# beta1 times the features: summed in PSUM by a product with a scaled identity, and z written by ScalarE

## The chip, the cores and the metric

One core of one Trainium2 chip runs the kernel. The metric is the device time of one execution in microseconds, the median of several runs. Engine names as in the profile: PE is TensorE (PEld its weight loads), DVE is VectorE, ACT is ScalarE, POOL is GpSimd, SP is SyncE. A letter L with a number is a line of the kernel before.

## What is computed

32 entries of 512 nodes with 256 features each, one adjacency matrix `adj` of 512 x 512 for all of them, four graph layers in a row, all in f32. Cut to what matters:

```
# layer 0 and, with other weights, layer 3 (B entries, h_t is [B, 512, 256])
pre_u, pre_v = h_t @ W1[:d], h_t @ W1[d:]
hidden = relu(pre_u[:, :, None] + pre_v[:, None] + b1)       # for every pair u, v
S = sigmoid(hidden @ W2 + b2)
a_t = einsum('buv,bud->bvd', S * A, h_t)                     # A = adj
m_t = einsum('uv,bud->bvd', A, h_t) * h_t
z_t = beta1 * h_t + beta2 * (a_t @ Wa + ba) + beta3 * (m_t @ Wm + bm)
# layer 1
z + relu((A @ z) @ W.T + b)
# layer 2: attention of all nodes, softmax(leaky_relu(f1_i + f1_j) + A), + input
```

The change is in the last line of layer 0, the sum z_t.

## The kernel before

`adj` is sparse, and the pair term `hidden` is needed only where `adj` is not zero. The kernel counts the nonzeros, and since they fit, takes the sparse path (`Sparse`); `dense_path` stands for other inputs and does not run here.

The 32 entries go in eight groups of four (`NB = 4`), and each group passes through these stages:

- `first`: transposes the features (hT), computes pre_u and pre_v and writes them as rows of a table in memory (L587).
- `edges` for layer 0 and again for layer 3: 36 blocks a group (`ITEMS`). For each block POOL gathers 128 rows of the table (L612), DVE adds the other side's rows (L691) and does relu and the weighting by W2. For every second block DVE weights all four entries in one operation (L699), and ACT then sums each entry's part (L677, four ACTIVATEs a block); for the others DVE does weighting and sum in four operations (L707). Then come the sigmoid (L597 on ACT, L601 to L641 on DVE) and a scatter of the values to memory (L606, POOL). The row buffers are five, and a gather is issued three blocks ahead.
- `middle`: layers 0 to 2 for the four entries one after another (`middle_one`), and at its end pre_u and pre_v of layer 3.
- `last`: the sums of layer 3 and the output.

`middle_one` is where the change lies. The features stand transposed: feature on the partition, node along the row, in two halves of 128 features (`DC = 2`). For one entry:

1. mhT, that is (A^T h) * h transposed, from PE products and a DVE multiplication by hT (L755).
2. For each half c a bank of PSUM, pz, takes four products with hWa, which is h @ (beta2 Wa), and flat, the matrix S * A of this entry (L845).
3. For each half, ACT writes beta1 * hT + bias into zT (L850; zT is the same buffer as hT), PE adds two products with beta3 Wm to pz (L852), and DVE adds pz to zT (L853). zT is z_t, transposed.
4. zW = z @ W of layer 1: eight products, first those of half 0 and then those of half 1 (L866), brought out by two copies on ACT (L870). Then the products with adjT (called from L875, recorded as L45 with `adjT,zW`), relu on ACT (L876), and the sum with zT on DVE (L877). Layer 2 follows with feats (L888).

The stages of different groups are woven together: while the middle of group t runs, the edges of group t + 1 and of layer 3 of group t - 1, and `first` and `last` of neighbours, are issued between its pieces. `sparse_path` gives each stage's pieces a time, `weave` issues them in the order of these times, and at the places where a piece says that PE will have to wait (`yield True`) it puts in pieces of `first` or `last` as filler. The pieces' times are numbers in the source; the order in which each engine takes its instructions is fixed when the program is built. Each engine takes its own queue in that order. So L853 stands in DVE's queue between operations of the edge stage, and L870 and L850 stand in ACT's queue between sums L677.

The weights times their beta are made once, in `gnn_scaled`; `bcol` there is beta2 ba + beta3 bm as a column.

Of the kernel before, what the change touches and what calls it, by code (L numbers as in the profile page):

```python
# [8 lines left out]
F32 = mybir.dt.float32  # L9
BF16 = mybir.dt.bfloat16  # L10
I32 = mybir.dt.int32
AF = mybir.ActivationFunctionType
ALU = mybir.AluOpType
# [3 lines left out]
P = 128  # L17
# [30 lines left out]
class Model:  # L48
# [48 lines left out]
    def gnn_first(self, L):  # L97
        nc, a, const = self.nc, self.a, self.const
        w = {"L": L}
        w["W1"] = self.load(f"{L}_W1", [P, 2 * DC, D], a[f"{L}_W1"].rearrange("(c p) k -> p c k", p=P))  # L100
        w["b1bc"] = self.bcast(f"{L}_b1", D)
        w["W2bc"] = const.tile([P, D], F32, name=f"{L}_W2bc")
        nc.scalar.dma_start(w["W2bc"], a[f"{L}_W2"].rearrange("k o -> (k o)").partition_broadcast(P))
        w["b2"] = self.bcast(f"{L}_b2", 1)
        w["nb2"] = const.tile([P, 1], F32, name=f"{L}_nb2")
        w["bcol"] = const.tile([P, DC, 1], F32, name=f"{L}_bcol")
        if L == "L3_gnn":
            w["bbc"] = const.tile([P, D], F32, name=f"{L}_bbc")
        for key in ("Wa", "Wm"):
            w[key] = const.tile([P, DC, D], F32, name=f"{L}_{key}")  # L110
        return w
# [14 lines left out]

    def gnn_scaled(self, w, beta, biases):
        nc = self.nc
        for key, n in (("Wa", 2), ("Wm", 3)):
            nc.vector.tensor_scalar(w[key], w[key], beta[n], None, ALU.mult)  # L130
            col, bc = biases[key]
            if n == 2:
                nc.vector.tensor_scalar(w["bcol"], col, beta[n], None, ALU.mult)
                nc.vector.tensor_scalar(w["bbc"], bc, beta[n], None, ALU.mult)
            else:
                nc.vector.scalar_tensor_tensor(w["bcol"], col, beta[n], w["bcol"], ALU.mult, ALU.add)
                nc.vector.scalar_tensor_tensor(w["bbc"], bc, beta[n], w["bbc"], ALU.mult, ALU.add)
# [281 lines left out]
class Sparse:  # L419
# [25 lines left out]
    def psum(self):  # L445
        return self.ps.tile([P, N], F32, name="pst", tag="pst")
# [383 lines left out]
    def middle_one(self, g0, g3, b, i, SA, keep, given):  # L830
        nc, m, w = self.nc, self.m, g0.w
        act, small, psum = self.act, self.small, self.psum
        h, hT, hWa, flat = keep
        if given:
            hWa, mhT = given[b]
# [3 lines left out]
        zT = hT  # L839
        sums = []  # L840
        for c in range(DC):
            cs = slice(c * P, (c + 1) * P)
            pz = psum()
            for r in range(NC):
                nc.tensor.matmul(pz, hWa[:, r, cs], flat[:, r, :], start=(r == 0), stop=False)  # L845
            sums.append(pz)
            yield
        for c, pz in enumerate(sums):
            cs = slice(c * P, (c + 1) * P)
            nc.scalar.activation(zT[:, c, :], hT[:, c, :], AF.Identity, bias=w["bcol"][:, c, :], scale=w["beta1"])  # L850
            for d in range(DC):
                nc.tensor.matmul(pz, w["Wm"][:, d, cs], mhT[:, d, :], start=False, stop=(d == DC - 1))  # L852
            nc.vector.tensor_tensor(zT[:, c, :], zT[:, c, :], pz, ALU.add)  # L853
            yield c == DC - 1
        more = b < NB - 1
        if more:
# [4 lines left out]
        for d in range(DC):  # L861
            for c, pw in halves:
                for k in range(2):
                    cs = slice((c + k) * P, (c + k + 1) * P)
# [21 lines left out]
        for r in range(DC):  # L886
            for ic, pn in enumerate(pns):
# [4 lines left out]
                    start=(r == 0),  # L892
                    stop=(r == DC - 1),
# [37 lines left out]
        for c in range(DC):  # L931
            cs = slice(c * P, (c + 1) * P)
# [435 lines left out]
```

## Time and profile before

| what | value |
|---|---|
| runs shown | 3096.97, 3109.6, 3116.11 us; median 3109.6 |
| profiled execution | 3114.49 us, span 3112.8 us |
| PE busy | 2713.5 us, 87% of the span |
| DVE busy | 2302.9 us, 74% |
| POOL busy | 1531.2 us, 49% |
| ACT busy | 1337.7 us, 43% |
| mean granted PE clock | 0.942 |
| L850 (ACT, 64 times) | 0.810 us each |
| L853 (DVE, 64 times) | 0.678 us each |
| L876 (ACT out of PSUM, 64 times) | 0.682 us each |

Busy is the time in which an engine has an instruction in it. A row of the timeline gives the start, the length, engine and line, the tile written and those read, how many instructions were merged, and in brackets how long the engine stood idle before it and what ended that. A row of the waits gives who waited for whom, the sum in us, how many times, and the longest. One f32 product appears as two instructions on PE.

The middle of the first group begins at about 235 us (the first L845 is at 239.8), and the last middle ends at 2889 us. Up to the first the setup and the first edge stage run, and behind the last the edge stage of layer 3 for the last group. Between them an entry of `middle_one` takes 80 to 94 us, measured from one entry's first L845 to that of the next, in the groups that run with other stages beside them.

### The profile page before, as it was taken

The numbers are of one execution on the slowest core, as the hardware profiler recorded it, in microseconds if no ns is written. First come the engines' busy times: TensorE is split into PE (matmuls) and PEld (weight loads), VectorE is DVE, ScalarE is ACT, GpSimd is POOL, SyncE is SP. The second block draws the span as 40 slices with busy tenths as digits, with TensorE's granted clock in tenths as the row PEclk, the third lists the DMA queues.
The fourth block names the chain that finished last, engine by engine and source line by source line (L and its number), as shares of the span: only waits on it lengthen the run. The fifth ranks groups of instructions, "written<-read, shape, count | busy, mean of one in ns | idle before, by whom it ended". The sixth has DMA issues, their size and how long they took to land. (4 is left out here: it accounts for less than half of the span.)

```text
span 3112.8 us, 32475 instructions
## 1 busy us (share of the span) xinstructions
PE 2713.5 (87%) x8645; PEld 1639.7 (53%) x8646; DVE 2302.9 (74%) x6027; ACT 1337.7 (43%) x4101; POOL 1531.2 (49%) x1328
## 2 busy tenths in 40 slices
PE   6367878889998899989998899989998899879957
PEld 3133444446654566446654565545654466546636
DVE  6964877888689776988489785888679795772761
ACT  3553454444344433444354442544345343443440
POOL 2561553656345552656346562555436563450461
PEclk9688889999999999999999999999999999999979
DMA  8774657776778757776678766787578766551753
GB/s 278 267 238 151 210 164 242 248 261 214 225 214 293 220 189 227 245 263 216 210 212 258 236 196 211 243 266 234 177 225 273 247 220 200 182 183 49 231 196 115
DMA packets 302719, 679.40 MB, mean 218 GB/s; under 512 B 52672, under 2 KB 170944, under 8 KB 294336
## 3 DMA queue, kind: packets, MB, share of 16 engines
q0 software_dynamic: 122688, 414.40, 42.6%
q1 hardware_dynamic: 160880, 225.62, 22.0%
q10 hardware_dynamic: 18960, 37.24, 3.2%
q8 instruction: 70, 1.15, 0.1%
q14 instruction: 121, 0.99, 0.1%
HBM read 531.12 MB, written 146.01 MB: 218 GB/s over the span
## 5 line engine op out<-in xcount | busy, mean ns | idle before, releaser
L606 POOL DMA_INDIRECT cells<-s,cell x576 | 686.4, 1192 | 747.0 <-DMA cells<-s,cell 388.5
L612 POOL DMA_INDIRECT rows<-table,iv x552 | 667.6, 1209 | 619.9 <-DMA table<-puv 150.5
L691 DVE TENSOR_TENSOR rows<-rows,mine 128x1024 f32<-128x1024 f32 x552 | 667.4, 1217 | 191.7 <-DMA rows<-table,iv 173.3
L677 ACT ACTIVATE rows<-rows 128x256 f32<-128x256 f32 x1088 | 439.8, 407 | 506.6 <-DVE rows L699 477.3
L45 PE MATMUL pst<-adj,h 128*128 128x512 f32 x1024 | 452.6, 594 | 0.3 <-PE pst L946 0.3
L707 DVE SCALAR_TENSOR_TENSOR rows<-rows,L_gnn_W2bc 128x256 f32<-128x256 f32 x1120 | 415.0, 417 | 1.8
L45 PE MATMUL pst<-L_gnn_Wa,hT 128*128 128x256 f32 x1024 | 261.3, 406 | 104.8 <-DMA hT<-xT 56.2
L699 DVE SCALAR_TENSOR_TENSOR rows<-rows,L_gnn_W2bc 128x1024 f32<-128x1024 f32 x272 | 329.7, 1214 | 0.3
L45 PEld LDWEIGHTS pst<-adj,h 128*128 128x128 f32 x1024 | 193.4, 191 | 223.3 <-issue 219.4
L45 PEld LDWEIGHTS pst<-L_gnn_Wa,hT 128*128 128x128 f32 x1024 | 204.8, 205 | 151.8 <-issue 85.1
L45 PE MATMUL pst<-eT,feats 128*128 128x512 f32 x512 | 230.9, 604 | 13.0 <-ACT eT L958 13.0
L866 PE MATMUL pst<-WT,hT 128*128 128x256 f32 x512 | 155.1, 470 | 96.0 <-DVE hT L853 96.0
L45 PE MATMUL pst<-adjT,zW 128*128 128x512 f32 x512 | 227.7, 597 | 3.8 <-ACT zW L870 3.8
L1006 PEld LDWEIGHTS pst<-hWa,SA 128*128 128x128 f32 x896 | 213.8, 328 | 7.7 <-issue 4.1
L1006 PE MATMUL pst<-hWa,SA 128*128 128x256 f32 x896 | 216.8, 398 | 0.0
L814 ACT COPY flat<-SA 128x512 f32<-128x512 f32 x128 | 137.7, 1127 | 165.9 <-PE pst L45 83.7
L677 ACT ACTIVATION_READ_ACCUMULATOR rows<-rows 128x1 f32 x1088 | 205.4, 189 | 0.0
L845 PE MATMUL pst<-flat,hWa 128*128 128x512 f32 x448 | 196.8, 592 | 0.0
L866 PEld LDWEIGHTS pst<-WT,hT 128*128 128x128 f32 x512 | 121.4, 242 | 136.6 <-DVE hT L853 107.1
L579 DVE TENSOR_TENSOR puv<-pst,bc_L_gnn_b 128x256 f32<-128x256 f32 x256 | 104.4, 414 | 95.8 <-DMA table<-puv 58.6
L580 ACT COPY puv<-pst 128x256 f32<-128x256 f32 x256 | 93.5, 370 | 180.6 <-DVE puv L579 162.7
L45 PEld LDWEIGHTS pst<-eT,feats 128*128 128x128 f32 x512 | 97.2, 193 | 127.5 <-issue 109.4
(172 smaller groups left out, 3984.4 us busy)
## 6 DMA issues: line engine op xcount, KB each, us to landing
table<-puv SPq DMA_DIRECT2D x256, 256.0 KB, 5.7
SA<-cells POOLq DMA_DIRECT2D x64, 1024.0 KB, 7.2
h<-in_x_dram SPq DMA_DIRECT2D x64, 512.0 KB, 6.5
mine<-table SPq DMA_DIRECT2D x64, 512.0 KB, 5.5
hT<-xT SPq DMA_DIRECT2D x36, 512.0 KB, 5.0
h<-x2s SPq DMA_DIRECT2D x36, 512.0 KB, 4.4
xT<-hT ACTq DMA_DIRECT2D x32, 512.0 KB, 6.1
x2T<-yT SPq DMA_DIRECT2D x32, 512.0 KB, 5.5
```

What stands on the lines that cost most here:

```text
L45: nc.tensor.matmul(out, lhsT, rhs, start=(n == 0), stop=(n == len(pairs) - 1))
L579: nc.vector.tensor_tensor(puv[:, 0, :], pp[:, 0:D], w["b1bc"], ALU.add)
L606: self.nc.gpsimd.indirect_dma_start(out=g.cells[half], out_offset=bass.IndirectOffsetOnAxis(ap=at, axis=0), in_=s, in_offset=None)
L612: self.nc.gpsimd.indirect_dma_start(out=rows, out_offset=None, in_=g.table, in_offset=bass.IndirectOffsetOnAxis(ap=at, axis=0))
L677: self.behind(nc.scalar.activation(part, part, AF.Identity, accum_out=g.s[:, k, b : b + 1]))
L691: self.behind(nc.vector.tensor_tensor(rows, rows, other, ALU.add))
L699: nc.vector.scalar_tensor_tensor(by_entry, by_entry, 0.0, w2, ALU.max, ALU.mult)
L707: nc.vector.scalar_tensor_tensor(part, part, 0.0, w["W2bc"], ALU.max, ALU.mult, accum_out=at)
L814: self.nc.scalar.copy(flat[:, r, :], SA[r][:, :, b])
L845: nc.tensor.matmul(pz, hWa[:, r, cs], flat[:, r, :], start=(r == 0), stop=False)
L866: nc.tensor.matmul(pw[:, at], zT[:, d, cs], m.WT_1[:, d, :], start=(d + k == 0), stop=(d * k == 1))
L1006: nc.tensor.matmul(pz[:, k * D : (k + 1) * D], SA[r][:, cs, b], hWa[:, r, :], start=(r + k == 0), stop=False)
```

## The change

A constant is added for layer 0: `beta1_I`, the 128 x 128 identity times beta1, made once in `gnn_scaled`. In `middle_one` each bank pz starts with a product of `beta1_I` with the half of hT, so that beta1 * h is in the sum that PE makes. The ACTIVATE that wrote beta1 * hT + bias ahead of the sum, and the DVE sum behind it, are gone; in their place one ACTIVATE reads pz when its last product is in, adds the bias, and writes zT.

```diff
@@ gnn_first
-        if L == "L3_gnn":
+        if L == "L0_gnn":
+            w["beta1_I"] = const.tile([P, P], F32, name=f"{L}_beta1_I")
+        else:
             w["bbc"] = const.tile([P, D], F32, name=f"{L}_bbc")
@@ gnn_scaled
+        if "beta1_I" in w:
+            nc.vector.tensor_scalar(w["beta1_I"], self.ident, w["beta1"], None, ALU.mult)
@@ middle_one
         for c in range(DC):
             cs = slice(c * P, (c + 1) * P)
             pz = psum()
+            nc.tensor.matmul(pz, w["beta1_I"], hT[:, c, :], start=True, stop=False)
             for r in range(NC):
-                nc.tensor.matmul(pz, hWa[:, r, cs], flat[:, r, :], start=(r == 0), stop=False)
+                nc.tensor.matmul(pz, hWa[:, r, cs], flat[:, r, :], start=False, stop=False)
             sums.append(pz)
             yield
         for c, pz in enumerate(sums):
             cs = slice(c * P, (c + 1) * P)
-            nc.scalar.activation(zT[:, c, :], hT[:, c, :], AF.Identity, bias=w["bcol"][:, c, :], scale=w["beta1"])
             for d in range(DC):
                 nc.tensor.matmul(pz, w["Wm"][:, d, cs], mhT[:, d, :], start=False, stop=(d == DC - 1))
-            nc.vector.tensor_tensor(zT[:, c, :], zT[:, c, :], pz, ALU.add)
+            nc.scalar.activation(zT[:, c, :], pz, AF.Identity, bias=w["bcol"][:, c, :])
             yield c == DC - 1
```

## The prediction

> **What bounds the kernel now.** I read the page's busy shares first, then what TensorE waited for, then the timelines around the longest of those waits, entry by entry.
>
> ```profile
> PE 2713.5 (87%) x8645; PEld 1639.7 (53%) x8646; DVE 2302.9 (74%) x6027; ACT 1337.7 (43%) x4101; POOL 1531.2 (49%) x1328
> ```
>
> TensorE is the fullest queue, VectorE next. In six stretches of 360 us from 500 to 2660 us PE is busy 332 to 339 us each, so a longer PE queue has little room. The waits of PE, longest in total:
>
> ```profile
> PE pst L866 <- DVE hT L853: 96.0, 22, 9.5
> PE pst L45 <- DMA hT<-xT: 56.2, 4, 28.7
> PE pst L45 <- DMA hT<-x2T: 42.4, 4, 19.2
> PE pst L957 <- DVE ex L918: 41.0, 23, 8.3
> ```
>
> The first is the wait that the change takes aside: the products of z with WT_1 (L866) wait 22 times for VectorE's sum (L853), 96 us. The timelines show why VectorE was late, here in entry 10 (the third of its group of four); PE, then DVE, then ACT:
>
> ```profile
> 1008.69 3.60 PE L852 MATMUL pst<-mhT,L_gnn_Wm 128*128 128x512 f32 x8
> 1012.13 1.89 PE L45 MATMUL pst<-L_gnn_Wa,hT 128*128 128x256 f32 x8
> 1023.54 6.70 PE L866 MATMUL pst<-WT,hT 128*128 128x256 f32 x16 [9.53 <-DVE hT L853]
> 1030.08 1.89 PE L45 MATMUL pst<-L_gnn_Wa,hT 128*128 128x256 f32 x8
> 1031.81 7.03 PE L45 MATMUL pst<-adjT,zW 128*128 128x512 f32 x16
> ...
> 1021.67 1.22 DVE L691 TENSOR_TENSOR rows<-rows,mine 128x1024 f32<-128x1024 f32 x1 [9.14 <-DMA rows<-table,iv]
> 1022.81 0.68 DVE L853 TENSOR_TENSOR hT<-hT,pst 128x512 f32<-128x512 f32 x1
> 1028.13 1.22 DVE L691 TENSOR_TENSOR rows<-rows,mine 128x1024 f32<-128x1024 f32 x1 [1.44 <-DMA rows<-table,iv]
> 1029.27 1.22 DVE L699 SCALAR_TENSOR_TENSOR rows<-rows,L_gnn_W2bc 128x1024 f32<-128x1024 f32 x1
> ...
> 1029.07 0.59 ACT L870 COPY zW<-pst 128x512 f32<-128x512 f32 x1 [14.41 <-PE pst L866]
> 1030.52 0.42 ACT L677 ACTIVATE rows<-rows 128x256 f32<-128x256 f32 x1 [0.87 <-DVE rows L699]
> 1032.13 0.56 ACT L870 COPY zW<-pst 128x512 f32<-128x512 f32 x1
> ```
>
> L853 stands in VectorE's queue behind a gathered block of the edge stage (L691), and that block's DMA landed late. It is not arithmetic that is slow: L853 itself takes 0.68 us. And L866 took 6.70 us for 16 instructions, where after no wait it takes 3.62: PE ran slow after standing still. The wait repeats by place in the group (the gaps before L866 from the PE timeline, entries 4 to 31): first entries mostly 2.8 to 5.7 us, second 3.7 to 3.9, third 5.0 to 9.5, fourth none.
>
> **Two rules of the skill.** The Trainium skill, "TensorE: Matmul & The Clock Gate", section "What's actually happening", says that PE's clock is halved when it has been idle for a while and comes back after some 3.4 us of work. The trace agrees: after a gap of 2.84 us L866 steps at 216 ns, after gaps of 3.3 us or more at 427 ns for up to 13 instructions (some 5.8 us with the first, longer than the page's figure; I go by the trace). Over all L866 groups the steps above 216 ns sum to 39 us, so I count stall and clock apart: 96 + 39 us hang on this wait. "Perfetto Trace Analysis", "Tensor Engine Instruction (MATMUL, LD_WEIGHTS)", says that ACT and DVE take their instructions strictly in order; the L853 row above (late behind L691 though its product had long ended) shows that for DVE, and the forecast uses it for ACT.
>
> **The change, part by part.**
> 1. TensorE, added: 64 products (32 entries, two halves) of 128x512. One f32 product is two instructions (L845: 512 instructions for 256 products), and L845 steps at 429 ns, so 0.86 us each, 1.72 us an entry, 55 us in all. They stand first in the PSUM group and need only hT, which L755 has already used: no new wait.
> 2. VectorE, removed: 64 x 0.678 us (L853) = 43 us, 1.36 us an entry.
> 3. ScalarE: 64 x 0.810 us (L850, out of SBUF) go, 64 come that read PSUM with a bias; nearest row L876, the same shape out of PSUM, 0.682 us. 8 us less on an engine 43% busy: nothing. What matters is its place: the wait for DVE's mhT (L850, 71.8 us of ACT idling) goes, one for PE's last L852 comes. Behind it stand the sums L677.
> 4. Setup: one VectorE operation of 128x128; an L707 of twice that width takes 0.42 us. Nothing.
>
> So the question is where PE waits next. In the order of the changed program I counted, for each entry, how many groups of sums (L677, one group to a gathered block) stand ahead of the new ACTIVATE and ahead of zW's copies (L870), and read in the trace when those sums ended. PE's order is otherwise unchanged around it. The ACTIVATE stands ahead of the late block, so z is ready in time nearly everywhere. But both copies of zW now stand one group of sums later in third entries: before, the first copy stood ahead of that group.
>
> *Third entries (6, 10, 14, 18, 22, 26).* Entry 10: PE would reach the adjT products at 1014.0 + 1.72 + 3.45 (L866) + 1.7 (filler) = 1021; the sums ahead of zW end at 1032.2 in the trace (their L691 at 1028.13 waits for its own DMA, so VectorE's saved time does not help); the copy ends 0.7 later, 1032.9. Before, these products began at 1031.81. So 1.1 us later, and now they, not L866, run at half clock: the slow time of about 5.8 us costs half of itself, 2.9. Sum +4.0. The same reading gives +4.6, +3.8, +4.4, +5.1 for entries 6, 14, 18, 26 and about +3 for entry 22: **+25 us**. The added products vanish in the wait; the wait itself stays, one step further on.
>
> *First entries.* Entry 20: arrival 1914.2 + 1.72 = 1915.9, sums ahead end 1916.4, z at 1917.1, L866 at 1917.2, not 1918.0: 0.8 gained, a stall of 1.3 that leaves the clock full, 3.0 more. Entries 12, 16, 24 give -3.6, -2.3, -0.9; entry 4 is held by zW (-1.1), entries 8 and 28 had no stall (+1.7, +1.5): **-8.5 us**. VectorE has room: it idles 2.8 us for PE at L877 in these.
>
> *Second entries.* PE gains about 2.1 + 2.4 - but VectorE is busy 82.3 to 82.6 of 86 to 88 us in entries 9, 13, 17, 25, so PE waits for it a little later (L957). I count only VectorE's own 1.4 us in five entries, +1 in entry 5, nothing in 29: **-6 us**.
>
> *Fourth entries.* PE never waits in them and VectorE idles 28 to 32 us: 7 x 1.72 = **+12 us**.
>
> *First group (0 to 3).* Waits of 0, 1.7, 0.9, 0: **+4.2 us**.
>
> Sum: 25 - 8.5 - 6 + 12 + 4.2 = +26.7 us. The profiled execution took 3114.5 us (span 3112.8), so 3141; the median of the runs shown is 3109.6, 4.9 less, so **3136 us**, 0.85% more.
>
> Bounds: what the trace does not show is the gathers' pace once PE runs differently. If the third entries' blocks come as before but the clock survives, +25 becomes +8; if second entries get all of PE's gain, -6 becomes -22. Both give 3136 - 33 = 3103. If first and second entries gain nothing and pay 1.72 each, +26.7 becomes 25 + 12 + 4 + 24 = 65: 3175.
>
> **The rivals.**
> *A, faster: the wait really goes.* Mechanism: in third entries the blocks ahead of zW come some 11 us earlier, because ScalarE no longer idles 71.8 us behind mhT and gives row buffers back sooner (POOL waited 70.4 us for L677). Then all 96 + 39 is won and 55 paid: 3109.6 - 80 = 3030. It decides when the sums ahead of zW end before PE gets to the adjT products (1021 in entry 10, they end at 1032). Against: the block was issued only when POOL was done waiting for scatters to land ahead of an SA load (4.02 us), which the change does not touch.
> *B, slower by the full product cost.* 55 us on a full PE and new waits as long as the old: 3165. For: PE is 93% busy from 500 to 2660. Against: stalls at that very place swallow a part.
> *C, no change.* Gathers and VectorE pace the loop, PE's 55 us fill its idle time, VectorE's 43 us help a little: 3110, within 15. For: PE idles 399 us of the span. Against: fourth entries have no idle PE.
> *D, the new ACTIVATE is not where it should be.* In the built order it follows directly on sums that end before z is due; excluded but for two or three entries.
>
> **How the numbers follow.** Forecast 0.55, C 0.16, B 0.16, A 0.13. The forecast alone is 3115 to 3155. A difference of about 1% is what a measurement of this kernel can tell from none. Slower by more than that is over 3141: a little under half of the forecast (0.26) and B (0.16), 0.42. Faster is A, 0.13; the rest, 0.45, is within 1%. The range runs from 3095 (the lower bound, with some of A) to 3165 (B).
>
> **What would show it.** Right: L866's wait falls from 96 to below 25 us; PE waits appear at the adjT products for zW (L870), 8 to 12 us long, once in a group, with those products slow behind them; PE busy up by some 40 us; fourth entries longer by 1.7 us; the same row waits (L691) of 8 to 9 us. Wrong: zW's copies not waiting for sums in third entries (A), or second entries shorter by over 3 us (VectorE was not the limit), or waits growing elsewhere in first entries.

## The result, and the profile after

The changed kernel took 3147.9 us (median of 4 runs, 3140.4 to 3156.4), the kernel before 3111.0 in the same job: ratio **1.0147, 95% interval 1.0121 to 1.0173**. That is slower by 37 us; the forecast was 3136 us, and its terms added up to 26.7 us more. The profiled execution has a span of 3143.8 us, 31.0 more than before; the mean granted clock is 0.941 for 0.942. Lines of the kernel after stand four further down (L866 is L870, L870 is L874, L691 is L695, and so on); the new product is L848, the new ACTIVATE L857.

The page's busy line after:

```profile
PE 2758.8 (88%) x8773; PEld 1653.3 (53%) x8774; DVE 2270.7 (72%) x5964; ACT 1324.0 (42%) x4101; POOL 1540.8 (49%) x1328
```

PE is busy 45 us longer (forecast: some 40 visible) and still has 12% of the span idle, so the added work alone doesn't explain the time. What PE waited for (total us, times, longest):

```profile
PE pst L45 <- ACT zW L874: 52.7, 7, 12.2
...
PE pst L961 <- DVE cols L921: 38.3, 6, 11.4
PE pst L961 <- DVE ex L922: 32.6, 14, 6.8
...
PE pst L870 <- ACT hT L857: 6.2, 3, 2.9
```

The wait of the products with WT_1 has gone, from 96.0 us to 6.2. In its place PE waits before the products with adjT, for zW. Entry 10 again (third of its group), PE, DVE and ACT of the kernel after:

```profile
1032.81 3.62 PE L870 MATMUL pst<-WT,hT 128*128 128x256 f32 x16
1036.26 1.89 PE L45 MATMUL pst<-L_gnn_Wa,hT 128*128 128x256 f32 x8
1047.36 8.74 PE L45 MATMUL pst<-adjT,zW 128*128 128x512 f32 x16 [9.21 <-ACT zW L874]
...
1036.91 1.23 DVE L695 TENSOR_TENSOR rows<-rows,mine 128x1024 f32<-128x1024 f32 x1 [8.99 <-DMA rows<-table,iv]
...
1042.26 1.23 DVE L695 TENSOR_TENSOR rows<-rows,mine 128x1024 f32<-128x1024 f32 x1 [1.40 <-DMA rows<-table,iv]
1043.40 1.22 DVE L703 SCALAR_TENSOR_TENSOR rows<-rows,L_gnn_W2bc 128x1024 f32<-128x1024 f32 x1
...
1031.28 0.69 ACT L857 ACTIVATE hT<-pst,L_gnn_bcol 128x512 f32<-128x512 f32 x1 [1.03 <-PE pst L856]
1044.65 0.42 ACT L681 ACTIVATE rows<-rows 128x256 f32<-128x256 f32 x1 [12.68 <-DVE rows L703]
...
1046.74 1.06 ACT L874 COPY zW<-pst 128x512 f32<-128x512 f32 x2
```

z is written early (1031.28) and L870 runs without a wait at full clock, 3.62 us. But both copies of zW (1046.74) stand behind a group of sums L681 (1044.65), and VectorE reaches the weighting that those sums need (1043.40) only behind the same late gathered block (8.99 us) that z waited for before, and the next one (1.40 us). PE stands still for 9.21 us and then runs the adjT products slowly, 8.74 us for 16 where before it took 7.03. This much went as forecast.

Time by place in the group tells the rest. The table has the mean length of an entry (from its first product with flat to that of the next entry), entries 8 to 27, five at each place, read from the PE timelines; "before" has two columns, the profile shown and that of a second run of the same kernel (the first experiment):

| place | before, two runs | after | after less their mean |
|---|---|---|---|
| first | 89.7, 88.9 | 87.0 | -2.3 |
| second | 87.2, 87.7 | 91.6 | +4.2 |
| third | 88.2, 85.9 | 90.3 | +3.3 |
| fourth | 92.0, 90.9 | 92.0 | +0.6 |

The sum is +5.7 us a group (357.1 and 353.4 before, 360.9 after), and second entries carry most of it. The forecast had them shorter. In a second entry PE's waits add up to 12.5 us after the change and to 11.6 and 10.6 us in the two runs before. So of the 4.2 us some 1.4 are more waiting, though the wait for z is gone; 1.7 are the product's own time, which the waits do not swallow here; and the other 1.1 are slower steps of PE (7.3 us a second entry over what the same steps take at full clock, and 5.4 and 6.9 us in the two runs before).

### The profile page after: what moved, and what is told of

It is laid out like the page before. It is cut to its first block, busy times and chain, and to the rows that moved or that the text cites. A ratio compares the mean times of both kernels' runs of the same rounds, so it can differ in the third digit from the quotient of the medians.

```text
span 3143.8 us, 32632 instructions
## 1 busy us (share of the span) xinstructions
PE 2758.8 (88%) x8773; PEld 1653.3 (53%) x8774; DVE 2270.7 (72%) x5964; ACT 1324.0 (42%) x4101; POOL 1540.8 (49%) x1328
## 3 DMA queue, kind: packets, MB, share of 16 engines
q8 instruction: 71, 1.16, 0.1%
## 5 line engine op out<-in xcount | busy, mean ns | idle before, releaser
L610 POOL DMA_INDIRECT cells<-s,cell x576 | 693.7, 1204 | 769.8 <-DMA cells<-s,cell 369.0
L695 DVE TENSOR_TENSOR rows<-rows,mine 128x1024 f32<-128x1024 f32 x552 | 667.3, 1218 | 237.1 <-DMA rows<-table,iv 218.2
L681 ACT ACTIVATE rows<-rows 128x256 f32<-128x256 f32 x1088 | 440.3, 407 | 673.0 <-DVE rows L703 641.2
L45 PE MATMUL pst<-adjT,zW 128*128 128x512 f32 x512 | 238.9, 622 | 61.9 <-ACT zW L874 52.7
L681 ACT ACTIVATION_READ_ACCUMULATOR rows<-rows 128x1 f32 x1088 | 205.5, 189 | 0.0
L45 PEld LDWEIGHTS pst<-adjT,zW 128*128 128x128 f32 x512 | 101.3, 200 | 187.7 <-issue 120.4
L579 PE MATMUL pst<-w_L_gnn_W,hT 128*128 128x512 f32 x256 | 140.0, 674 | 37.7 <-ACT hT L566 20.0
```

What stands on the lines that cost most here:

```text
L45: nc.tensor.matmul(out, lhsT, rhs, start=(n == 0), stop=(n == len(pairs) - 1))
L579: nc.tensor.matmul(pp, hT[:, 0, ks], w["W1"][:, 0::DC, :], start=True, stop=False)
L610: self.nc.gpsimd.indirect_dma_start(out=g.cells[half], out_offset=bass.IndirectOffsetOnAxis(ap=at, axis=0), in_=s, in_offset=None)
L681: self.behind(nc.scalar.activation(part, part, AF.Identity, accum_out=g.s[:, k, b : b + 1]))
L695: self.behind(nc.vector.tensor_tensor(rows, rows, other, ALU.add))
```

## Experiments

Twelve kernels; each ratio is against the kernel before on the same chip, with its 95% interval.

**1. The kernel before again**, to see how far two profiles of one program differ.

> The kernel before, unchanged, for a second trace of it. Ratio 1.000 within 0.003. Every theory: the wait of L866 for L853 is 90 to 100 us again, in first, second and third entries, none in fourth. If the two short groups of the first trace (entries 8 to 11 and 24 to 27, 350 us against 360 for the others) are chance, other groups are the short ones here.

1.0013 (0.9998 to 1.0029). Its groups differ from the first profile's by up to 10 us; single entries are compared as means over five only, and differences of a place below some 2 us are not read.

**2. The product alone.** A product of a zero matrix with hT is put first in each bank, z stays on ScalarE and VectorE:

```diff
+            nc.tensor.matmul(pz, w["none"], hT[:, c, :], start=True, stop=False)
```

> The kernel before with one product more per bank, of a zero matrix with hT, so 55 us more for TensorE and everything else as it was. Theory 1 (an added product costs only in entries where TensorE does not wait anyway): 12 us from fourth entries, 4 from the first group, 2 to 8 from third entries, whose first copy of zW falls one group of sums later in the built order here too: 18 to 25 us, ratio 1.006 to 1.008. Rival B (TensorE is full): 55 us, 1.018. Rival C (the chain of gathers and scatters paces a group of four): 0 to 8 us, below 1.003.

1.0012 (0.9999 to 1.0026): a miss for my theory. 55 us of PE work cost about 4 us, no more than the unchanged kernel differed from itself in run 1. First entries got shorter with it, 87.0 us for 89.3: in the kernel before, four of the five stand 2.8 to 3.7 us at L866, and behind the longer three of these waits it runs slowly; here the product fills that time and no wait is left. Why the block that held z also comes earlier there isn't settled.

**3. ScalarE's part alone.** The new ACTIVATE without the product; z leaves out beta1 * h.

```diff
-            nc.scalar.activation(zT[:, c, :], hT[:, c, :], AF.Identity, bias=w["bcol"][:, c, :], scale=w["beta1"])
-            nc.vector.tensor_tensor(zT[:, c, :], zT[:, c, :], pz, ALU.add)
+            nc.scalar.activation(zT[:, c, :], pz, AF.Identity, bias=w["bcol"][:, c, :])
```

> The changed kernel without its product: beta1 times h is left out of z, ScalarE writes z out of PSUM. Theory 1 (the wait moves from L866 to the products with adjT in third entries, and what first entries gain is given back in second ones): between -10 and +10 us, ratio 0.997 to 1.003, with 50 to 60 us of waiting for zW. Rival B (the product is all that the change costs, 55 of TensorE against 37 measured): -18 us, 0.994. Rival A (the wait is gone): -80 us.

1.0050 (1.0022 to 1.0078). The wait for zW is here too, 74.9 us.

**4. The product, with VectorE writing z.** As after, but z = pz + bias by one VectorE operation:

```diff
-            nc.scalar.activation(zT[:, c, :], pz, AF.Identity, bias=w["bcol"][:, c, :])
+            nc.vector.tensor_scalar(zT[:, c, :], pz, w["bcol"][:, c, :], None, ALU.add)
```

> The changed kernel with VectorE in ScalarE's place: z = pz + bias by one VectorE operation, the product kept, no ScalarE operation on z. Theory 1 (as in the run with the product alone: the wait for VectorE at L866 is back, the product lies in it): 15 to 25 us, 1.005 to 1.008, so some 15 us below the changed kernel. If ScalarE's place in the queue costs nothing, it is as slow as the changed kernel: 37 us, 1.012 or more.

1.0013 (1.0000 to 1.0026). Same products, same PE work as after, but none of the loss: entries 87.0, 86.1, 87.9, 92.0. So in this order of the queues the loss of the changed kernel hangs on z being written by ScalarE and not by VectorE, and the product adds to it only then (1.0050 without it, 1.0147 with it).

**5 and 6. The order of ScalarE's queue.** In the order built for the changed kernel, the second relu of y and the copies of feats in second entries stand behind one more group of sums than before. I took that for the cause. `behind` orders an instruction of the edge stage behind the middle stage's last instruction but one on its engine; here sums and block adds follow the last one, which puts relu and feats one group earlier again. Run in the changed kernel and, as a control, in the kernel before:

```diff
-    def behind(self, ins):
+    def behind(self, ins, back=2):
-        if len(names) > 1 and names[-2]:
+        if len(names) >= back and names[-back]:
-            self.tc.add_manual_dep(ins.ins, names[-2], order, reason="behind the middle stage")
+            self.tc.add_manual_dep(ins.ins, names[-back], order, reason="behind the middle stage")
-                self.behind(nc.scalar.activation(part, part, AF.Identity, accum_out=g.s[:, k, b : b + 1]))
+                self.behind(nc.scalar.activation(part, part, AF.Identity, accum_out=g.s[:, k, b : b + 1]), 1)
-            self.behind(nc.vector.tensor_tensor(rows, rows, other, ALU.add))
+            self.behind(nc.vector.tensor_tensor(rows, rows, other, ALU.add), 1)
```

> The changed kernel with the edge stage's sums (ScalarE) and block sums (VectorE) ordered behind the last piece of the middle stage instead of the last but one. In the built order the second relu and the feats copies of second entries then stand behind one group of sums less, as in the kernel before; third entries keep both copies of zW behind the late group. Theory 2 (the 4 us that second entries lost are this place in ScalarE's queue): 18 to 28 us below the changed kernel, 1.004 to 1.009 of before, second entries back at 87 to 88 us. Rival (the product's time on TensorE is what second entries pay): second entries stay at 91 to 92 us, 1.012 to 1.015.

> The same order rule in the kernel before, as a control of the rule alone. The wait for L853 in third entries is untouched, the relu and sum of y stand one or two blocks earlier. Theory 2: -10 to +5 us, 0.997 to 1.002. If the rule by itself is worth as much as in the changed kernel (18 us or more), the run with the changed kernel says nothing of the changed kernel's own place in the queue.

1.0071 (1.0043 to 1.0099) and 0.9970 (0.9954 to 0.9986). Second entries fell to 88.5 us. That looked like a confirmation; runs 11 and 12 undid it.

**7 and 8. The sums ahead of zW held back.** Besides the order of 5 and 6, in third entries the sums between z and zW are issued one block later:

```diff
+        self.hold = b == 2
...
-            if summed:
+            if summed and self.hold:
+                late.append(summed.pop(0))
+            elif summed:
                 summed.pop(0)()
```

> As the changed kernel with that order rule, and in third entries the one group of sums that comes between z and zW is issued a block later, so that both copies of zW stand ahead of the late group. Theory 2 (in third entries the wait for the late block was handed from z to zW by ScalarE's queue): the wait of the adjT products for zW falls from 53 us to under 10, third entries are 4 to 7 us shorter than with the rule alone, 25 to 40 us in all: 0.992 to 1.001 of before. Rival (the late block holds third entries up wherever it is waited for): no more than 5 us below the run with the rule alone, with a new wait at the next products, for y.

> Both order edits in the kernel before, the control of the run above. VectorE's sum for z stands behind the late block there, so the copies of zW cannot come early: within 0.003 of the kernel before with the rule alone, by theory 2 and by the rival alike.

1.0163 (1.0133 to 1.0193) in the changed kernel, a miss, and 0.9947 (0.9922 to 0.9972) in the kernel before. PE's waits in run 7 (its line numbers; L888 adds z to y, L968 turns the attention weights):

```profile
PE pst L968 <- DVE ex L929: 72.7, 31, 8.9
...
PE pst L899 <- DVE yT L888: 35.0, 14, 4.7
```

The wait for zW is gone, and PE waits two steps further, at y and at the attention weights; third entries grew to 94.3 us. The late block is waited for wherever its work next stands ahead of the middle stage. In the kernel before, the same hold did no harm (0.9947, and 0.9970 without it in run 6).

**9 and 10. Which half of the change costs under the order of 5 and 6.** Run 9 is the kernel of run 4, run 10 that of run 3 (z leaves out beta1 * h), both with that order:

> The product of beta1 stays, VectorE writes z out of PSUM, ScalarE has no part in it, and sums and row adds follow the last mark (the order rule of the e5 and e6 runs, 1.0071 and 0.997). Theory 1, the forecast's own terms hold once the order is fixed and add up: the product alone costs its 1.72 us in fourth entries (12 us in all), so 1.000 to 1.003, fourth entries 92.0 us, third entries at about 86 us as in e6, because L870 waits for VectorE and zW does not. Rival, the two parts cost only together: 0.995 to 0.998, what fourth entries lose comes back in first ones (87 us instead of 89).

> ScalarE writes z from PSUM, without the product (z leaves out beta1*h), and sums and row adds follow the last mark. Theory 1, terms add up: third entries pay for the wait on zW as in e5 (about 90 us against 86 in e6, some 28 us in all), first and second entries as e6 or a little shorter, fourth 90.3 us: 1.002 to 1.006. Rival, the two parts cost only together: 0.996 to 0.999, third entries at 86 to 88 us.

1.0115 (1.0093 to 1.0137) and 1.0001 (0.9988 to 1.0013). Both miss both of their theories: run 10 lies between its two ranges, with third entries of 87.1 us and second ones of 91.9; run 9 lies far above, and third entries took 93.4 us. Its DVE and PE in entry 18:

```profile
1784.97 1.23 DVE L695 TENSOR_TENSOR rows<-rows,mine 128x1024 f32<-128x1024 f32 x1 [6.68 <-DMA rows<-table,iv]
...
1793.68 1.12 PE L961 MATMUL pst<-ident,ex 128*128 128x128 f32 x4 [4.26 <-DVE ex L922]
```

One block later than the one that z waits for, VectorE stands 6.68 us for a gather with the softmax behind it. The costs of the parts don't add up, and which part costs more turns round with the order of the queues (runs 3 and 4 against 10 and 9).

**11 and 12. The order mended in second entries alone**, from y to the copies of feats; ScalarE's order in all other entries stays that of the changed kernel.

```diff
-                self.behind(nc.scalar.activation(part, part, AF.Identity, accum_out=g.s[:, k, b : b + 1]))
+                self.behind(nc.scalar.activation(part, part, AF.Identity, accum_out=g.s[:, k, b : b + 1]), 1 if self.near else 2)
-            self.behind(nc.vector.tensor_tensor(rows, rows, other, ALU.add))
+            self.behind(nc.vector.tensor_tensor(rows, rows, other, ALU.add), 1 if self.near else 2)
+        self.near = b == 1
         yT = act.tile([P, DC, N], F32, name="yT")
...
+        self.near = False
         fcol = small.tile([P, NC, 1], F32, name="fcol", bufs=1)
```

> The changed kernel with the order rule of e5 only in second entries, from y to the copies of feats: there the second relu of y and the copies of feats stand one group of sums earlier again, as in the kernel before; the order of ScalarE in all other entries stays that of the changed kernel. Theory 1, the place in ScalarE's queue costs second entries 3.5 us each and nobody takes that gain away: second entries at 87 to 88.5 us instead of 91.6, the others as in the changed kernel (87, 90, 92), seven groups 25 us shorter, ratio 1.005 to 1.009. Rival, the gathers and VectorE pace the group, as the run with the product and VectorE's z under the near rule (1.0115) lets one suspect: second entries get shorter, but third or first entries get longer by as much, 1.011 to 1.016.

> Control: the same edit in the kernel before, where ScalarE's second relu of y and feats already stand at that place; it moves a block add behind the sum for y in second entries on VectorE. Theory 1: 0.997 to 1.003. Rival: the moved block adds alone change the pace, below 0.996 or above 1.004, in which case e11 is to be read against this run and not against the kernel before.

1.0130 (1.0103 to 1.0156) and 1.0013 (0.9999 to 1.0026): the rival. Second entries took 90.5 us, not 87 to 88.5, and third ones 91.5. Where the time went is seen in entry 17 of run 11 (DVE, ACT, PE):

```profile
1697.01 1.23 DVE L696 TENSOR_TENSOR rows<-rows,mine 128x1024 f32<-128x1024 f32 x1 [3.75 <-DMA rows<-table,iv]
...
1699.53 0.42 ACT L682 ACTIVATE rows<-rows 128x256 f32<-128x256 f32 x1 [4.28 <-DVE rows L704]
...
1702.43 0.59 ACT L567 COPY hT<-pst 128x512 f32<-128x512 f32 x1
...
1703.07 3.78 PE L582 MATMUL pst<-w_L_gnn_W,hT 128*128 128x512 f32 x4 [4.93 <-ACT hT L567]
```

feats no longer waits, but the block is late all the same; now the copy of the next features (L567) stands behind its sums, and PE waits 4.93 us there. ScalarE's place in second entries was not the cause by itself: with the place mended, PE waits for the late block one step further on.

**Why the block is late.** POOL of the kernel before in entry 17 (which begins at 1632.2), then VectorE, then PE's transposes of the next features and ScalarE's issue of the transfer that writes these to memory:

```profile
1650.66 1.16 POOL L612 DMA_INDIRECT rows<-table,iv  x1 [0.30 <-DVE hT L853]
...
1653.40 1.00 POOL L606 DMA_INDIRECT cells<-s,cell  x1 [0.30 <-DVE rows L691]
...
1656.01 0.99 POOL L612 DMA_INDIRECT rows<-table,iv  x1 [0.30 <-ACT zW L870]
1660.68 1.04 POOL L606 DMA_INDIRECT cells<-s,cell  x1 [3.69 <-DMA cells<-s,cell]
...
1650.89 0.67 DVE L853 TENSOR_TENSOR hT<-hT,pst 128x512 f32<-128x512 f32 x1
...
1655.92 1.04 PE L561 MATMUL pst<-ident,h 128*128 128x128 f32 x8
...
1657.72 0.33 ACTq L773 DMA_DIRECT2D xT<-hT  x1
```

and of the kernel after (the entry begins at 1648.4), with two of VectorE's later waits:

```profile
1665.12 1.75 POOL L616 DMA_INDIRECT rows<-table,iv  x1 [0.30 <-DVE both L587]
...
1668.45 1.00 POOL L610 DMA_INDIRECT cells<-s,cell  x1 [0.30 <-issue]
1669.76 1.66 POOL L610 DMA_INDIRECT cells<-s,cell  x1 [0.30 <-issue]
1671.72 1.60 POOL L616 DMA_INDIRECT rows<-table,iv  x1 [0.31 <-issue]
1677.03 1.33 POOL L610 DMA_INDIRECT cells<-s,cell  x1 [3.71 <-DMA cells<-s,cell]
...
1664.78 1.22 DVE L695 TENSOR_TENSOR rows<-rows,mine 128x1024 f32<-128x1024 f32 x1
...
1669.32 1.22 DVE L695 TENSOR_TENSOR rows<-rows,mine 128x1024 f32<-128x1024 f32 x1
...
1671.23 1.23 DVE L695 TENSOR_TENSOR rows<-rows,mine 128x1024 f32<-128x1024 f32 x1 [0.69 <-DMA rows<-table,iv]
...
1685.50 1.22 DVE L695 TENSOR_TENSOR rows<-rows,mine 128x1024 f32<-128x1024 f32 x1 [2.01 <-DMA rows<-table,iv]
...
1691.83 1.23 DVE L695 TENSOR_TENSOR rows<-rows,mine 128x1024 f32<-128x1024 f32 x1 [2.96 <-DMA rows<-table,iv]
...
1666.48 1.04 PE L565 MATMUL pst<-ident,h 128*128 128x128 f32 x8
...
1669.06 0.33 ACTq L777 DMA_DIRECT2D xT<-hT  x1
```

POOL issues gathers and scatters one after another. The scatter in the last POOL line waits until the one three issues ahead of it (1653.40 and 1668.45) has landed, and the gathers of the next blocks stand behind it. Two things differ.

First, POOL's issues. Before, they take 0.99 to 1.16 us; the first one shown lies beside the sum of z (L853). Without z, VectorE takes up its block adds (L695) earlier, three issues of POOL start while one runs, and take 1.60 to 1.75 us. But only the first of the three stands ahead of the scatter that is waited for. The other two are issued while it is on its way, in time in which POOL would only wait longer.

Second, the landing of that scatter: 7.0 us from its issue before, 8.3 after. With no wait for z, PE comes to the next features' transposes 18.1 us into the entry and not 23.7. These set off two transfers of 512 KB each, the write shown (xT) and a read of h on SP's queue. Before, none of that write moves before the scatter has landed; after, all of it does:

```profile
1653.40:1660.40 7.00, 6.71 (x27) 4.37 (x26) 6.41 (x18) 2.66 (x6) 2.99 (x3) 0.94 0.92 275
...
1668.45:1676.70 8.25, 8.10 (x19) 3.72 (x20) 6.91 (x19) 3.13 (x12) 4.26 (x3) 1.00 0.97 354
```

(From the scatter's issue to its landing, before and after; the last two figures are the DMA engines' busy share and the GB/s that they moved.) Over all runs, means of the five second entries from entry 9 to 25:

| z is written by | runs | landing of the scatter waited for, us | wait for it, us | second + third entry, us |
|---|---|---|---|---|
| VectorE | before, 1, 2, 4, 12 | 6.9, 6.6, 6.5, 6.6, 6.5 | 3.5, 3.0, 3.2, 3.3, 3.2 | 175.4, 173.6, 176.2, 174.1, 175.9 |
| VectorE, sums near | 6, 8, 9 | 4.6, 4.6, 6.3 | 1.1, 1.2, 3.0 | 174.0, 174.7, 181.2 |
| ScalarE | after, 3, 11 | 8.7, 8.8, 9.0 | 4.3, 4.2, 4.8 | 182.0, 180.2, 182.0 |
| ScalarE, sums near | 5, 7, 10 | 8.1, 7.9, 8.8 | 4.7, 4.5, 5.4 | 179.2, 181.8, 179.0 |

("Sums near" is the order of run 5.) In all 30 of these entries in the six kernels in which ScalarE writes z, the whole write of xT moved between that scatter's issue and its landing, which took 7.6 to 9.7 us. In the 40 entries of the eight other kernels none of it did, but for half of it in one (entry 13 of run 2), and the landing took 4.4 to 7.1 us. (In runs 6 and 8 less of POOL's own traffic lies in that time, 0.57 MB for 1.3, so their 4.6 us is no measure for the other rows.) From the gather that POOL issues some 12 us into the entry to the scatter that waits it is 15.6 to 16.0 us in the first row and 18.3 to 18.6 in the third. Of these 2.6 us, the slower issue ahead of the awaited scatter makes 0.5, and its landing makes 2.1. (POOL's nine issues in that stretch take 1.5 us longer in sum, 10.1 and 11.6, but 1.0 of it lies in the wait.) In the last row the issues are not longer, only the landing is.

So it is shown that POOL's chain is later, by 2 to 4 us against the kernels with VectorE's z in the same order of the queues, in all six kernels in which ScalarE writes z, and that the early transfers come with it each time. That these slow the scatter fits all 70 entries but is read from the timelines: no run held them back alone. How much of PE's loss the late chain makes isn't settled either. Run 9 shows that second and third entries can lose as much by another way, with neither the early transfers nor the slow landing.

## Why the forecast was right in part, and where it failed

- *The wait moves from z to zW in third entries, +25 us.* Right in mechanism. L870's wait is 6.2 us, the waits for zW are 7.6 to 12.2 us in six third entries. The size in the steady entries is +3.3 us an entry, or +2.1 against the first profile alone, for +4.2 forecast. The slow clock cost 2.3 us (the five steady entries lost 1.7, 2.9, 1.8, 3.1 and 2.1 to steps over 429 ns), not 2.9: with the steps of these larger products the slow time lasted 3.4 to 6.1 us, so it begins at the figure that the Trainium skill gives on "TensorE: Matmul & The Clock Gate", "What's actually happening", and goes beyond it. The line that the prediction drew between gaps of 2.84 us, which left the clock full, and of 3.3 us is not a rule: in run 4 gaps of 1.9 to 2.3 us (entries 9, 13, 17 and 25) were followed by eight steps of about 427 ns, which began 0.5 to 1.5 us after the gap had ended.
- *First entries, -8.5 us.* Right in sign, and more of it: -2.3 us each in the steady entries (-15 us over seven against the first profile), since they came down to PE's own floor of 87.0 us.
- *Second entries, -6 us.* **This is the step that failed.** It said that PE gains there and that VectorE, busy 82 of 86 to 88 us, gives back only its own 1.4 us. It took every gather to land when it did before. Measured: +4.2 us each, +24 us over seven entries against the first profile, a turn of 30 us. The wait for z went, as forecast, but PE's waits came back elsewhere in the entry and grew by 1.4 us, and so they didn't swallow the product's 1.7. The gathers landed later: from 33 to 50 us into these entries VectorE waits 2.0 to 5.4 us for them, and not at all before but for 1.4 us in one entry of ten over the two runs. POOL's chain was late, most likely because PE's own gain let other transfers start earlier. The forecast had named the gathers' pace as what the trace of before can't show, but put its bound on PE's side only.
- *Fourth entries, +12 us.* The term of 1.72 us is exact as a floor: 90.3 us without the product (runs 6, 8 and 10), 92.0 with it (after, 2, 4, 9 and 11). But in the kernel before not all of them were at that floor (means of 92.0 and 90.9). The forecast read that PE never waits there; in the first profile three of five waited 1.8 to 2.3 us at their end. So the price was 0.6 us each, some 4 in all.
- *First group, +4.2 us.* Twice that, and not where it was forecast: entry 4 starts 8.6 us later than in the first profile, some 8 later than in the mean of both, and 7.9 of it is there when entry 1 starts. In entry 0 the new product waits 8.0 us for hT's own transfer ("PE pst L848 <- DMA hT<-xT: 8.0, 1, 8.0" among PE's waits), where the forecast said that it brings no new wait. Before, PE waited 12.6 us for flat at that place, and what makes up the rest isn't settled.
- Of the signs named ahead, L870's wait, the waits for zW, PE's +45 us and the row waits (8.99 us) came; "fourth entries longer by 1.7 us" did not.
- *Rivals.* A fell: zW waits for the sums. B's full product cost fell in run 2: 55 us of PE work cost 4. D fell with L870's wait of 6.2 us. C's claim that gathers pace the loop was nearer to the truth than I gave it, but the pace wasn't the same as before. That the total came out near the forecast is luck in good part. Against the first profile the terms are, forecast and measured: first group +4 and +9, first entries -8.5 and -15, second -6 and +24, third +25 and +13, fourth +12 and +2, and the end, not forecast, -1. They are missed by 4 to 30 us each, and the misses nearly cancel.

Two orders of the kernel before beat both kernels: run 6 (0.9970) and run 8, **0.9947 (0.9922 to 0.9972)**, both with sums and block adds in the order of run 5, and run 8 with the sums ahead of zW held back besides. They leave z as it was.

## What to carry to other kernels

Taking a wait away moves all that stands behind it in the queue, transfers too: ask not only who waits for the engine but what it will now set off earlier, and what that runs into. A gain in PE's queue here started 1 MB of transfers 4 to 5 us earlier into the entry, just while a scatter that the next gathers stood behind was on its way. Where a late transfer sets the pace, moving the instruction that waits for it, or mending the order at one place, hands the wait to the next in the queue; compare the length of the whole stretch that the transfer sets, not that of the wait. Change one half of an edit at a time in both directions (with and without the other half): here, in the built order of the queues, neither half alone cost more than 0.5%, and together they cost 1.5%.

## What the hardware showed beside this

POOL's issue of an indirect DMA depends on what VectorE is doing when it starts. Between 500 and 2600 us of the kernel before it took 977 ns (median of 89) with no VectorE operation beside it, and 980 ns (23) beside operations that read one operand from PSUM, such as L579, L582 and L853. Where it started while L691 or L699 had over 0.6 us to run, which read both operands from SBUF, it took 1700 ns (186); where such an operation started within 0.2 us after it, 1000 ns (58). After the change the four are 978, 971, 1706 and 1004 ns. VectorE pays nothing: these operations take 1216 and 1217 ns (medians) with and without an issue of POOL running at their start. The Trainium skill, "SBUF — State Buffer", "Who interferes with whom", draws the same line (two SBUF inputs contend with a GpSimd instruction that reads SBUF; at most one, outside VectorE's 2-port modes, doesn't), and says that the first to issue blocks the other; of the two directions only the one in which POOL waits is seen here. What the section infers besides, that `tensor_tensor` does not stall the generation of descriptors, does not hold for these issues.
